# Moving the head, the softmax and the first projections of an attention layer, and ending its last block and the last row in halves of 256 tokens

## The chip, the cores and the metric

One NeuronCore of a Trainium2 chip runs the whole program. The metric is device time in microseconds for one execution. Engines are named as in the profile: PE (TensorE matmul), PEld (its weight loads), DVE (VectorE), ACT (ScalarE), POOL (GpSimd), SP (SyncE, which here only issues DMAs). Each engine works through its own list of instructions in order and waits for others by semaphores.

## The reference, cut to what matters

Four transformer layers over 2048 tokens of width 128, all float32. The kernel cuts the tokens into four rows ("b") of 512. The parts that matter here:

```
x = x + 0.5 * L0_ffn(layernorm(x))        # top-2 of 8 experts + a shared one
x = x + L0_attn(layernorm(x))             # 16 heads of 64, rope on q and k
x = x + 0.5 * L0_ffn(layernorm(x))
... layers 1 and 2, first half and attention of layer 3 ...
x = x + 0.5 * L3_ffn(layernorm(x))        # last thing computed

L0_attn(x):  h = layernorm(x) * ln_scale + ln_bias
             c_q, c_kv = h @ w_down_q.T, h @ w_down_kv.T        # 64 wide
             q, k, v   = c_q @ w_up_q.T, c_kv @ w_up_k.T, c_kv @ w_up_v.T
             q, k      = rope(q), rope(k)
             out       = softmax(q k.T / 8) v @ w_out.T + x
L3_ffn(x):   xr, xk = mu * x + (1 - mu) * x_of_the_token_before
             out    = sigmoid(xr @ W_r.T) * (relu(xk @ W_k.T)**2 @ W_v.T)
```

## The kernel before

**Stages.** The first mixture of experts sorts the tokens of all rows by expert into DRAM (`sorted_x`), works through tiles of 128 sorted tokens two at a time (`tiles`, lines 689 to 787: transpose L713, up L723, product L730, limits L732/L736, L737, L739, transpose L748, down L756, store L760), and gathers the results back per row (`back`, an indirect DMA on POOL at L804 and an add at L799). Layer 0's attention (`l0_attn_quick`) follows, then the second mixture, and so on up to the attention of layers 2 and 3 (`padded_attn_quick`) and the last layer's channel mix (`l3_ffn`).

**Layer 0's attention.** 32 steps, four rows of eight pairs of heads. A step computes the scores of its pair in four tiles of 128 keys (L1032, two 512-wide matmuls each), their exponentials on ACT (L1033 into `pT`), the products with the values (L1046), the running sums for the softmax's denominators on DVE (L1038, L1041: three 1024-wide additions) and a copy of the result on ACT (L1118 into `U`). Between the third and the fourth score tile it also projects the pair two steps ahead (L1014 on PE, copy L1016 on ACT into `qk`, then two DMAs L1019 that write the pairwise swapped rows into `other`) and turns the pair one step ahead on DVE (two multiplications by the rope table at L1024, an addition at L1025). The first two projections and the first turn stand ahead of the loop, at lines 1074 and 1075; their tiles come from the pool `work` of this stage.

Three further streams are generators, of which a `yield` ends a piece; the loop runs one piece in the middle of a step and one at its end:

- `l0_begin(b + 1)`, the head of the next row: two layer norms, the projections `w_down` to `cT` (L989 on PE, copy L991 on ACT) and V (L995, L997). It is appended at the end of the step `hp == NP - 6`, the third of the row; whatever is left of it runs in full before the first projection of the next row (`finish(chain(*begins))`), in the seventh step.
- `end(b)`: the sums of the denominators (L1052), the reciprocal (L1054), `watch` (L962, one pass that looks for overflow), spreading over partitions (L1062), four multiplications of `U` (L1064), the projection `w_out` (L1069) and the addition to x (L321).
- `late(b)`, the routing of a finished row for the second mixture: layer norm, transposes (L310), gate logits (L484), the softmax over 8 experts (`exps`, L354 to L357), ranks (L333 to L338), `taken` (L493), counts on PE (L500, L502), places, and eight indirect DMAs.

**Order of the work.** In this stage PE's list is exactly the order in which the code issues (`manual_schedule` on PE). The lists of DVE, ACT, POOL and SP are ordered by a scheduler that estimates times. PSUM holds three `big` tiles of two banks and two `one` tiles; a pool of the next stage lies over the memory of the last one (`reuse_waits="tile"`), so the first writer of a tile waits for the last users of what lay there.

**The last row.** In `padded_attn_quick` the step `end(k, U)` (L1465 denominators, L1467 reciprocal, L962, L1474, L1476, L1481) is followed for the last row by `l3_ffn` (layer norm L286 to L299, transposes L310, copy L1772, token mix L1778/L1779, L1784, L1786, L1788, L1791, L1792, L1796, L1797, L1798, and the store L1800), each operation over all 512 tokens.

Of the kernel before, what the change touches and what calls it, by code (L numbers as in the profile page):

```python
# [238 lines left out]
def program(ctx: ExitStack, tc: tile.TileContext, a: dict, out: bass.AP, worst):  # L239
# [193 lines left out]
    def by_expert(w, rooms, key):  # L433
# [33 lines left out]
        def route(b, work, rows_pool=None, slow=False):  # L467
# [6 lines left out]
            yield  # L474
# [8 lines left out]
            for t in range(NT):  # L483
                nc.tensor.matmul(lg[:, t, :], lhsT=xnT[:, t * P : (t + 1) * P], rhs=w["gate_w"], start=True, stop=True)  # L484
            sc = exps(lg, NT)
# [491 lines left out]

    def l0_begin(b, w, work, made, bufs):

        xa = keep.tile([P, NT, D], F32, tag="xn", name="xa", bufs=3)  # L980
        yield from layernorm_parts(x[b], xa)
        nc.gpsimd.tensor_tensor(x[b], x[b], xa, ALU.add)
        yield from layernorm_parts(xa, xa)
        yield
        hT = keep.tile([P, S], F32, tag=f"xnT{b}", name=f"hT{b}")
        nc.vector.tensor_scalar(hT, transposed(xa), w["ln_scale"], w["ln_bias"], ALU.mult, ALU.add)
        yield
        pd = one()
        nc.tensor.matmul(pd, lhsT=w["w_down"], rhs=hT, start=True, stop=True)  # L989
        cT = work.tile([P, S], F32, tag="cT", name="cT", bufs=bufs)  # L990
        nc.scalar.copy(cT, pd)  # L991

        pv = one()
        for t in range(NT):
            nc.tensor.matmul(pv[:, t * 64 : (t + 1) * 64], lhsT=hT[:, t * P : (t + 1) * P], rhs=w["w_down"][:, 64:128], start=True, stop=True)  # L995
        V = work.tile([P, NT, 64], F32, tag="V", name="V", bufs=bufs)
        nc.vector.tensor_copy(V.rearrange("p t d -> p (t d)"), pv[:, : NT * 64])  # L997
        made[b] = cT, V
        yield

    def l0_attn_quick(w, work, made, early, late):

        rope = w["c_rope"].rearrange("p (m s) -> p m s", m=2)
# [5 lines left out]

        def project(hp, cT):  # L1010

            pq = big()
            for k, row in enumerate((0, 64)):
                nc.tensor.matmul(pq[:, k, :], lhsT=w["w_up_qk"][row : row + 64, hp * P : (hp + 1) * P], rhs=cT[row : row + 64, :], start=True, stop=True)  # L1014
            qk = work.tile([P, 2, S], F32, tag="qk", name="qk", bufs=3)
            nc.scalar.copy(qk, pq)  # L1016
            other = work.tile([P, 2, S], F32, tag="other", name="other", bufs=2)
            for m in range(2):
                nc.sync.dma_start(out=other[m::2], in_=qk[1 - m :: 2])  # L1019
            return qk, other  # L1020

        def turned(qk, other):
            for v, m in ((qk, 0), (other, 1)):
                nc.vector.tensor_tensor(v, v, rope[:, m, :].unsqueeze(1).to_broadcast([P, 2, S]), ALU.mult)  # L1024
            nc.vector.tensor_tensor(qk, qk, other, ALU.add)  # L1025
            return qk[:, 0, :], qk[:, 1, :]
# [21 lines left out]
        def end(b, U, sums):  # L1048
# [5 lines left out]
            nc.vector.reciprocal(r, pz)  # L1054
            watch(b, pz, r)
            yield
            for k in range(2):
                for c2 in range(2):
                    pr = big()
                    for m in range(2):  # L1060
                        c = 2 * c2 + m
                        nc.tensor.matmul(pr[:, m, :], lhsT=spread[32 * c : 32 * c + 32, k, :], rhs=r[32 * c : 32 * c + 32, :], start=True, stop=True)  # L1062
                    u = U[k][:, 2 * c2 : 2 * c2 + 2, :]
                    nc.vector.tensor_tensor(u, u, pr, ALU.mult)  # L1064
                yield
# [8 lines left out]
        raw = {n: project(n, made[0][0]) for n in range(2)}  # L1074
        qk = {0: turned(*raw[0])}
# [14 lines left out]
        for n, (b, hp) in enumerate(todo):  # L1090
# [6 lines left out]
            for half in range(2):  # L1097
                pTs.append(work.tile([P, 2, 2, S], F32, tag="pT", name="pT", bufs=3))
                for t in (2 * half, 2 * half + 1):
                    if t == NT - 1 and n + 1 < len(todo):  # L1100
                        if n + 2 < len(todo):
                            b1, hp1 = todo[n + 2]
                            if hp1 == 0:
                                finish(chain(*begins))
                            raw[n + 2] = project(hp1, made[b1][0])
                        qk[n + 1] = turned(*raw[n + 1])
                    score(t, *qk[n], pTs[half])
# [21 lines left out]
            if b + 1 < B and hp == NP - 6:  # L1129
# [267 lines left out]
    def padded_attn_quick(rows, w, work, before, side):  # L1397
# [85 lines left out]


# [6 lines left out]
        for r in range(2 * len(todo) + 1):  # L1491
# [8 lines left out]
            if r:  # L1500
# [11 lines left out]
                if h1:  # L1512
                    nc.vector.tensor_copy(U[:, g1, :], po)  # L1513
                    if g1 == NG - 1:
                        ends.append(end(k1, U))
                        step(ends[0])
# [9 lines left out]
        finish(chain(*ends))  # L1526
# [293 lines left out]
    with tc.tile_pool(name="w0", bufs=1, reuse_waits="tile") as wp:  # L1820
# [9 lines left out]
        else:  # L1830
# [13 lines left out]
            with tc.tile_pool(name="work", bufs=1, reuse_waits="tile") as work:  # L1844
# [25 lines left out]
                first, second = chain(places, mix.back(0, wp), l0_begin(0, w0, head, made, 1)), mix.back(1, wp)  # L1870
# [15 lines left out]
            with tc.tile_pool(name="work", bufs=1, reuse_waits="tile") as work:  # L1886
                with tc.manual_schedule(engines={mybir.EngineType.PE}):
                    rest = l0_attn_quick(w0, work, made, [iter(())] + [mix.back(b, wp) for b in range(2, B)], lambda b: mix2.route(b, wp, slow=(b < B - 1)))
# [21 lines left out]
    with tc.tile_pool(name="w13", bufs=1, reuse_waits="tile") as wp:  # L1910
# [50 lines left out]
        else:  # L1961
            deep[0] = 3
            rows = [(n, b, causal) for n, causal in (("l2", True), ("l3", False)) for b in range(B)]
            with tc.tile_pool(name="work", bufs=1, reuse_waits="tile") as work:
# [11 lines left out]
                plan += [(4 + b, 8, channels(True, b)) for b in range(B)]  # L1976
# [21 lines left out]
                padded_attn_quick(rows, wa, work, before, side)  # L1998
                before(8)
# [17 lines left out]
```

## Time and profile before

| | |
|---|---|
| runs before | 1462.82, 1467.87, 1468.65 us; median 1467.87 us |
| profiled execution | 1463.96 us, span 1462.2 us, mean granted clock of PE 0.927 |
| PE / DVE / ACT / POOL busy | 87% / 66% / 44% / 19% of the span |
| layer 0's attention, first score to the last row's `w_out` | 213.5 to 581.8 us |
| last row, from the last copy into `U` to the store's issue | 1421.7 to 1451.1 us |

The profile is one execution. Its page gives busy shares of each engine, the span cut into 40 slices, the chain of work that ended last, and groups of instructions by line. A busy share is an average: what an edit is worth is read at its place, from which wait ends last there. "PEclk" is the share of its full clock that PE was granted.

### The profile page before, as it was taken

Reading aid. Unit: us, or ns where it says so; the run is one execution under the profiler, and the core shown is the slowest. Engines: PE = TensorE matmul, PEld = TensorE weight load, DVE = VectorE, ACT = ScalarE, POOL = GpSimd, SP = SyncE. Lnnn points to the kernel's source line nnn. Section 1 sums busy time; section 2 is a strip of 40 time slices with the busy share of each in tenths; the row PEclk is TensorE's granted clock in tenths of the full one; section 3 lists DMA queues with packets and bytes.
Section 4 is the critical chain, followed back from the end, with each engine's and each line's share of the span. In section 5 each row is a group of like instructions: output and inputs, shape, how many; then the busy total and the mean of one; then the engine's idle time right before and its main releaser. Section 6 shows DMA issues by size and latency. Waiting matters only on the chain.

```text
span 1462.2 us, 20126 instructions
## 1 busy us (share of the span) xinstructions
PE 1271.6 (87%) x7044; PEld 672.8 (46%) x7044; DVE 963.8 (66%) x2331; ACT 645.8 (44%) x920; POOL 284.6 (19%) x270
## 2 busy tenths in 40 slices
PE   6999879998999999999876598789897889899983
PEld 3555543343344434555544385453464445333322
DVE  4796769988888794977675646467666634364423
ACT  2445446544444451555543242434343445445550
POOL 3510420203112020202343212220213030210000
PEclk9999999999999998999996697799898999899996
DMA  7123111101111010022115000010010000000000
GB/s 271 42 72 98 52 63 73 72 29 57 65 44 59 29 67 25 30 62 64 30 37 178 1 1 1 30 30 1 7 31 22 1 14 24 22 1 15 1 8 10
DMA packets 59953, 63.52 MB, mean 43 GB/s; under 512 B 11066, under 2 KB 51267, under 8 KB 59203
## 3 DMA queue, kind: packets, MB, share of 16 engines
q1 hardware_dynamic: 54212, 50.60, 10.2%
q0 software_dynamic: 5632, 11.55, 2.7%
q8 instruction: 59, 0.97, 0.3%
q14 instruction: 50, 0.41, 0.1%
HBM read 28.69 MB, written 16.65 MB: 31 GB/s over the span
## 4 chain that ended last, share of the span: by engine, by line
PE 65%; DVE 17%; issue 8%; ACT 4%; POOL 3%; DMA 2%; SPq 0%; POOLq 0%; ACTq 0%; DVEq 0%
PE big L1032 7%; PE big L1446 6%; PE big L723 6%; PE one L1046 6%; PE one L1459 5%; PE big L568 3%; PE one L1069 2%; ACT pT L1449 2%; PE one L1481 2%; PE big L1014 2%; PE one L310 2%; PE one L756 2%; POOL rs L290 1%; PE big L1720 1%; PE one L1734 1%
## 5 line engine op out<-in xcount | busy, mean ns | idle before, releaser
L1449 ACT ACTIVATE pT<-big 128x1024 f32<-128x1024 f32 (+3 forms) x256 | 205.0, 866 | 235.5 <-PE big L1446 232.6
L1446 PE MATMUL big<-qkq,qkk 32*128 32x512 f32 (+3 forms) x1024 | 176.5, 580 | 23.8 <-ACT pT L1449 13.2
L290 POOL TENSOR_TENSOR rs<-rs,root 128x4 f32<-128x4 f32 x52 | 58.0, 1117 | 501.3 <-DVE rs L289 474.6
L1033 ACT ACTIVATE pT<-big 128x1024 f32<-128x1024 f32 x128 | 125.9, 1034 | 66.0 <-PE big L1032 65.1
L723 PE MATMUL big<-w_w,xsT 128*128 x312 | 152.0, 610 | 0.7 <-issue 0.3
L1032 PE MATMUL big<-qk 64*128 64x512 f32 x512 | 129.8, 624 | 12.5 <-DVE qk L1025 7.3
L1459 PE MATMUL one<-pT,V 128*32 128x512 f32 (+3 forms) x1024 | 121.3, 561 | 1.3 <-DVE pT L1453 0.9
L1046 PE MATMUL one<-pT,V 128*64 128x512 f32 x512 | 116.9, 598 | 0.0
L1446 PEld LDWEIGHTS big<-qkq,qkk 32*128 32x128 f32 x1024 | 64.3, 194 | 111.9 <-ACT pT L1449 43.9
L804 POOL DMA_INDIRECT yg<-sorted_y,ito x64 | 70.1, 1096 | 210.4 <-DMA sorted_y<-ys 152.4
L548 POOL DMA_INDIRECT sorted_x<-xn,irows x64 | 69.6, 1088 | 79.1 <-issue 22.0
L1032 PEld LDWEIGHTS big<-qk 64*128 64x128 f32 x512 | 47.9, 193 | 79.9 <-issue 54.0
L1041 DVE TENSOR_TENSOR sums<-sums,pT 128x1024 f32<-128x1024 f32 x64 | 78.2, 1221 | 5.7 <-ACT pT L1033 1.0
L1453 DVE TENSOR_TENSOR pT<-pT,w_c_tri 128x256 f32<-128x256 f32 x128 | 51.9, 422 | 35.4 <-ACT pT L1449 34.2
L723 PEld LDWEIGHTS big<-w_w,xsT 128*128 128x128 f32 x312 | 54.2, 194 | 39.4 <-issue 39.3
L1046 PEld LDWEIGHTS one<-pT,V 128*64 128x64 f32 x512 | 33.9, 136 | 73.6 <-issue 69.0
L1459 PEld LDWEIGHTS one<-pT,V 128*32 128x32 f32 x1024 | 29.5, 115 | 76.4 <-issue 55.6
L1513 DVE COPY U<-one 128x512 f32<-128x512 f32 x32 | 22.0, 689 | 63.9 <-PE one L1459 63.5
L730 DVE TENSOR_TENSOR us<-big,t1s 128x1024 f32<-128x1024 f32 (+1 forms) x40 | 47.7, 1193 | 24.0 <-PE one L713 20.4
L321 DVE TENSOR_TENSOR x<-x,one 128x512 f32<-128x512 f32 x32 | 21.9, 685 | 62.0 <-PE one L1069 19.5
L568 PE MATMUL big<-xnT,w_w 128*128 128x512 f32 x128 | 60.0, 607 | 2.1 <-DVE u L573 2.1
L1118 ACT COPY U<-one 128x512 f32<-128x512 f32 x32 | 18.8, 586 | 97.1 <-PE one L1046 97.1
(311 smaller groups left out, 2313.7 us busy)
## 6 DMA issues: line engine op xcount, KB each, us to landing
other<-qk SPq DMA_DIRECT2D x64, 256.0 KB, 2.4
xs<-sorted_x SPq DMA_DIRECT2D x78, 64.0 KB, 1.8
sorted_y<-ys SPq DMA_DIRECT2D x38, 128.0 KB, 1.8
w_w<-in_w SPq DMA_DIRECT2D x2, 2048.0 KB
w_l_w<-in_l_w SPq DMA_DIRECT2D x2, 2048.0 KB, 14.4
X<-pair_x SPq DMA_DIRECT2D x3, 512.0 KB, 3.6
pair_y<-y SPq DMA_DIRECT2D x6, 256.0 KB, 2.3
w_w<-in_w SPq DMA_DIRECT2D x1, 1152.0 KB, 15.0
```

The lines of the kernel that those rows point to most:

```text
L290: nc.gpsimd.tensor_tensor(rs, rs, root, ALU.pow)
L548: apart(nc.gpsimd.indirect_dma_start(out=sorted_x[:, :], out_offset=bass.IndirectOffsetOnAxis(ap=irows[:, b, j, t : t + 1], axis=0), in_=x ...
L568: nc.tensor.matmul(pa[:, m, :], lhsT=w["w13"][:, NE, m, odd, c * P : (c + 1) * P], rhs=xTs[b], start=True, stop=True)
L723: nc.tensor.matmul(pa[:, k, :], lhsT=st[u]["xT"][:, k * P : (k + 1) * P], rhs=w["w13"][:, bass.ds(st[u]["e"][k], 1), m].rearrange("p o a b ...
L804: nc.gpsimd.indirect_dma_start(out=y, out_offset=None, in_=sorted_y[: done(b) * P, :], in_offset=bass.IndirectOffsetOnAxis(ap=ito[:, b, j, ...
L1032: nc.tensor.matmul(sT[:, u, :], lhsT=k[r, t * P : (t + 1) * P], rhs=q[r, :], start=True, stop=True)
L1033: nc.scalar.activation(pT[:, :, t % 2, :], sT, AF.Exp, scale=scale)
L1041: nc.vector.tensor_tensor(s, s, pT[:, :, m, :], ALU.add)
L1046: nc.tensor.matmul(po[r, :], lhsT=V[:, t, :], rhs=pT[:, u, t % 2, :], start=(t == 0), stop=(t == NT - 1), tile_position=(0, 64 * u))
L1446: nc.tensor.matmul(sT[j // 2][:, j % 2, :n], lhsT=kT[r, t * P : (t + 1) * P], rhs=qT[r, S - n :], start=True, stop=True)
L1449: nc.scalar.activation(pT[j2][:, :, :n], sT[j2][:, :, :n], AF.Exp, scale=scale)
L1459: nc.tensor.matmul(po[32 * j : 32 * j + 32, S - n :], lhsT=V[k % 2][:, t, NJ * g + j, :], rhs=pT[j // 2][:, j % 2, :n], start=(t == 0), st ...
```

## The change

1. `project` and `turned` become `l0_project` and `l0_turned`, with their tiles `qk` and `other` in the pool `head`, which lives from before the first mixture. The first two projections and the first turn are issued as pieces of the chain that runs beside the first mixture's tiles, behind `l0_begin(0)`; the scheduler places the second pair's turn there too.
2. `l0_begin(b + 1)` is appended one step later (`NP - 5`), so its last piece falls to the forced finish ahead of the next row's first projection.
3. In a slow `route`, the piece boundary that stood between the layer norm and the transposes goes behind the gate logits: transposes and logits are each issued half a step earlier, and the softmax starts one piece after the logits.
4. In `end`, `watch` goes behind the multiplications; for the last row, the reciprocal, the spreading and the multiplications are done in two halves of 256 tokens.
5. For the very last row, `end` and `l3_ffn` are replaced by `end_all`, which does all of it in two halves of 256 tokens, and stores each half by its own DMA.

```diff
@@ route
             yield from layernorm_parts(x[b], xn)
-            yield
+            if not slow:
+                yield
             xnT = keep.tile([P, S], F32, tag=f"xnT{b}", name=f"xnT{b}")
 ...
+            if slow:
+                yield
             sc = exps(lg, NT)
@@ end of l0_attn_quick
             r = work.tile([P, S], F32, tag="rsum", name="rsum")
-            nc.vector.reciprocal(r, pz)
-            watch(b, pz, r)
+            N = S if b + 1 < B else S // 2
+            cols = [slice(n, n + N) for n in range(0, S, N)]
+            for n in cols:
+                nc.vector.reciprocal(r[:, n], pz[:, n])
             yield
-            for k in range(2):
-                for c2 in range(2):
 ...
+            for n in cols:
+                for k in range(2):
+                    for c2 in range(2):
 ...
+                    if k and n == cols[-1]:
+                        watch(b, pz, r)
+                    yield
@@ l0_attn_quick
-        raw = {n: project(n, made[0][0]) for n in range(2)}
-        qk = {0: turned(*raw[0])}
+        raw, qk = first
 ...
-            if b + 1 < B and hp == NP - 6:
+            if b + 1 < B and hp == NP - 5:
@@ padded_attn_quick
-                    if g1 == NG - 1:
+                    if g1 == NG - 1 and k1 + 1 < len(rows):
 ...
-        finish(chain(*ends))
+        before(len(rows))
+        end_all(len(rows) - 1, U)
@@ program, beside the first mixture's tiles
+                def projected():
+                    raw, qk = pair01
+                    for n in range(2):
+                        raw[n] = l0_project(n, made[0][0], w0, head)
+                        yield
+                    qk[0] = l0_turned(w0, *raw[0])
+                    yield
+
-                first, second = chain(places, mix.back(0, wp), l0_begin(0, w0, head, made, 1)), mix.back(1, wp)
+                first, second = chain(places, mix.back(0, wp), l0_begin(0, w0, head, made, 1), projected()), mix.back(1, wp)
```

The new `end_all`, shortened:

```
for c in cols:                       # two halves of 256 tokens
    pz = one(); 4 matmuls (pick); r[:, c] = 1 / pz; z[:, c] = pz (ACT)
for c in cols:
    for g2 in range(2): pr = big(); 2 matmuls (spread); U[..., c] *= pr
for i in range(2):                   # w_o, addition, statistics, POOL's power
    po = one(); 8 matmuls; x += po; bn_stats, bn_aggr x2; rs
for i in range(2):                   # normalise, transpose, copy
    xn (DVE x2); 2 transposes; xnT[:, half] (ACT)
for i in range(2):                   # token mix: 4 DVE operations
    ...
for i in range(2):
    pkr = big(); W_k (256 wide), W_r x2; relu and tanh (ACT); kT * kT (DVE)
for i in range(2):
    pv = one(); W_v x2; r, x (DVE); store of the half
watch(2 * B + b, z, r)
```

## The prediction

> **What bounds the kernel now.** I read the page first, then PE's waits inside layer 0's attention, then the chain of waits at the places that the change touches, then stretches around those places. The page gives the frame:
>
> ```profile
> PE 1271.6 (87%) x7044; PEld 672.8 (46%) x7044; DVE 963.8 (66%) x2331; ACT 645.8 (44%) x920; POOL 284.6 (19%) x270
> PEclk9999999999999998999996697799898999899996
> ```
>
> PE is the bound nearly everywhere, so an edit is worth the idle time of PE that it removes, plus what that idle time does to the clock. The waits of PE between 205 and 590 us, longest in total first:
>
> ```profile
> PE one L500 <- DVE taken L493: 8.8, 3, 4.2
> PE big L1032 <- DVE qk L1025: 7.3, 1, 7.3
> PE big L1062 <- DVE rsum L1054: 5.6, 4, 3.5
> PE big L1032 <- DVE U L1064: 5.2, 3, 1.7
> ```
>
> Each is a place of the change: the routing's counts waiting for the ranks, the first score waiting for the first turned pair, the spreading waiting for the reciprocal. The chain of waits shows the second and the last end, and the end of the program:
>
> ```profile
> 207.09 2.36 DMA other<-qk
> 213.51 5.05 PE big L1032 x12
> ...
> 562.36 3.37 DVE rsum L1054
> 565.77 5.16 PE big L1062 x16
> 570.93 2.86 PE one L1069 x12
> 573.79 1.71 PE big L568 x2
> 575.50 6.30 PE one L1069 x52
> ...
> 1422.85 3.37 DVE rsum L1467
> 1426.27 2.10 PE big L1474 x8
> 1429.67 5.63 PE one L1481 x32
> ```
>
> Stretches (columns: PE, PEld, DVE, ACT, POOL busy, then PEclk) show what idling costs afterwards:
>
> ```profile
> 340.90:344.30 3.40, 0.68 (x4) 0.00 (x0) 3.33 (x6) 0.58 (x1) 0.73 (x1) 1.00 0.05 19
> 344.30:351.10 6.80, 5.34 (x20) 3.98 (x22) 5.75 (x16) 0.00 (x0) 1.06 (x1) 0.50 0.04 10
> 887.00:890.40 3.40, 1.45 (x12) 1.36 (x12) 2.21 (x13) 0.69 (x1) 2.53 (x3) 1.00 0.00 0
> 890.40:897.20 6.80, 6.07 (x16) 3.35 (x14) 3.88 (x21) 0.58 (x1) 4.27 (x3) 0.50 0.02 4
> 323.60:360.00 36.40, 32.21 (x148) 14.60 (x146) 31.36 (x64) 16.89 (x21) 8.23 (x8) 0.91 0.14 51
> 1421.70:1451.10 29.40, 14.99 (x67) 9.94 (x66) 14.29 (x30) 1.67 (x3) 1.01 (x1) 0.75 0.00 1
> ```
>
> After 3.4 us with PE 0.68 us busy the clock is half for 6.8 us. The second pair of lines shows the same after 3.4 us with PE 1.45 us busy, 43%.
>
> **The change part by part.** Sums are against the profiled execution, 1463.96 us (3.9 below the median of the runs, 1467.87).
>
> *Entry of the attention (edit 1).* Removed: PE's wait of 7.29 us (206.22 to 213.51), made of the copy (1.02), the swap's issue and DMA (0.55 + 2.36), and the turn (1.23 + 1.15 + 1.24). It set the clock to half from 211.2 to 218.0; 4.5 us of scores ran in that, worth 2.2. Gross 9.5. The moved instructions all remain: on PE 1.99 us of L1014, on ACT two copies of 1.02, on SP four DMA issues ahead of later tile stores (L760, hidden: 0.56 each, the stores are waited for two units later at the earliest), on DVE six operations of 1.22, 7.3 us. From 169.0 to 206.2 PE was busy 36.3 of 37.2 us, DVE 25.6, ACT 16.8, so the room on DVE is 11.6 us. But DVE goes in order, and in the new list it stands at the first rope multiplication until the swap has landed. I place it: down-projection once hT is there (170.4), cT at 171.9, projection done near 174.2, copy to 175.2, swap landed near 178.4 (the old pair took 3.3 us from copy to L1024); the next tile product behind it (L730) has its matmuls only at about 180.8, so the wait and the first two multiplications just fit. From there five units of 3.5 us each, eight adds L799 of 0.33, four statistics, and 4.9 us of turning end DVE's last L739 near 208.2 instead of 201.2. PE, at its last L748, waits about 2 us for that, and loses 1.3 us earlier (the down-projection now directly follows the transposes L310 and waits for hT, where two L723 covered it). The first exponential, after the table load that stands in front of it (1.28), comes at about 211.4 instead of 216.95. Net 5.5. From both sides: 9.5 if DVE keeps up, 1 if every moved DVE microsecond lands on PE. I take 5.5, from the placing.
>
> *Routing and head (edits 2 and 3).* The waits at L500 are 4.19, 4.05 and 0.54 us, in rows 0, 1 and 2. They exist because from 333.3 to 341.6 DVE is full (8.30 of 8.30 us): the next row's second layer norm sits among softmax and ranks. With the softmax half a step earlier (into DVE's idle 2.34 us before L354) and the head a step later, I place `taken` at 337.8, ahead of L500 at 341.6. All 8.8 us go. So do the half clocks behind them: 5.35 and 5.7 us of PE work ran at half, worth 5.5. Gross 14.3. What is late next: the head's last piece is now forced ahead of L1014 in the seventh step. There L989 must be copied to cT (L991, 0.63) behind three running exponentials before L1014 can start; with exponentials ending 1.2 us behind the scores, PE waits 0.85 us in each of three rows, 2.6. It is covered only by L995 (0.5 to 1.0). DVE total in 323.6 to 360.0 is 31.4 of 36.4 us; without the gaps about 30 us of time remain there, so it fits only because the head's 5 us move behind 360, where DVE has 5.7 us free to 387.3. For such tightness I take off 1.
>
> *Ends of rows 0 to 2 (edit 4).* Taking `watch` (0.68 + 0.14) from behind the reciprocal frees the first multiplication 0.45 us sooner, but the scheduler now puts a rope multiplication (1.22) between the two: the second PSUM tile is freed 0.75 later, and the next multiplications about 1.3 later, which L1069 feels by 0.7. Bounds: gain 0.8 or loss 1.2 a row; I take a loss of 0.9, 2.7 in all. Edits 2 to 4 up to here: 14.3 - 2.6 - 1 - 2.7 = 8.
>
> *End of the last block (edit 4).* No row shows half sizes. A 512-wide L730 took 0.68, a 1024-wide one 1.22, so 256 more columns cost 0.27 and each instruction about 0.15. Half a reciprocal is then 1.75, half a multiplication 0.69. PE starts spreading at 564.1 instead of 565.8, but eight multiplications and `watch` (now third) end on DVE at 572.3, exactly as before. The last spreading needs a PSUM tile from the fifth multiplication, so L1069 starts at 570.7 instead of 570.9. What is gained: two L568 (1.71) leave the middle (0.9 comes back later at full clock), and some half clock (566.1 to 576.4 before). 1.5; bounds 0 and 3.6.
>
> *Last row (edit 5).* From the copy (1421.7) to the store (1451.1) were 29.4 us with DVE busy 14.3 and PE 15.0: a chain, hardly overlapped. In halves, by the same per-instruction costs: denominators to 1422.5, reciprocals to 1426.05, four multiplications with `watch` and the final check to 1430.05. With PE at full clock the first half's addition is at 1430.5, its normalised x at 1433.15 (POOL's 1.0 stalls DVE, with the other half queued behind it); the second half's addition 1433.6, POOL done 1436.2, transposes 1437.2, copy 1437.6, mix 1438.65, relu 1439.65, W_v 1441.1, end 1442.0: 9.1 saved. With PE at half, the second half's `w_o` ends at 1435.4 and the end is at 1444.85: 6.2 saved.
>
> **Two rules of the Trainium skill.** For the clock: "TensorE: Matmul & The Clock Gate", part 1, says half rate comes after one *idle* window of about 3.4 us. Halving leaves no idle window, so by the rule both ends run at full clock: 3.6 and 9.1. The row at 887.0 (43% busy, then half) says a half-busy window is enough, and both halved ends leave PE between 40 and 55% busy; by it 0.7 and 6.2. I go between, nearer the row: 1.5 and 7.5. Against the change, "VectorE: DVE Perf Modes", section on the TRN2 errata, advises tiles of 512 elements or more because each instruction pays a fixed latency. The 0.15 us above is that cost here; some 24 more DVE instructions in the two ends make 3.6 us if DVE were the bound throughout. In the last row it is busy half the time, so the rule costs only what the placing already contains; if obeyed (no halves), the two ends would bring 0.8 for the moved `watch` instead of 9.
>
> **Sum.** 5.5 + 8 + 1.5 + 7.5 = 22.5: 1441.5 us as the profiled execution counts. The runs shown lie up to 4.7 above it, so I put the forecast 1.5 higher, at 1443. No edit touches the stretch from 630 to 1405; it shifts as a whole, with clock windows falling elsewhere (2 us either way).
>
> **The rivals.**
>
> - *As summed* (0.65): 1435 to 1451.
> - *The clock stays full and nothing new waits* (0.12): entry 9.5, rows 14.3, ends 3.6 and 9.1, 36 at the most, some 30 likely: 1434. For it: PE's gaps at the ordinary ends (0.72 + 1.75 us) left the clock alone. Against: cT's wait follows from the order.
> - *DVE becomes the bound* (0.20): the moved turn lands on PE (1), DVE at 85% in the attention takes back most of the routing's gain (3), ends 0 and 6: 10 saved, 1454 to 1457, seen from the runs about 0.8% faster; with the tail at 4 it counts as the same.
> - *Slower* (0.03): the wait for the swap inside the tile loop. It is one DMA wait at the head of DVE's queue, with the tile products, L739 and so PE's L748 behind it. Beyond the 3.3 us that I took, each further microsecond costs one, since the cover up to 180.8 is used up. It decides from 22 us late; swaps here landed in 2.4 us each, tile stores in 1.8, so nothing speaks for it.
> - That the code does not do what it says: both programs' instruction lists show the first scores ahead of the last tile's L748, so it does.
>
> **How the numbers follow.** 0.5%, 7.3 us, is about what a measurement of this kernel can tell from no change (the runs spread over 5.8 us). Faster: 0.65 + 0.12 + 0.14 of the third case. Same: its remaining 0.06. Slower: 0.03. The range 1431 to 1455 takes in the first case with its bounds, most of the second and the better half of the third.
>
> **What would show it.** In the profile after: no PE wait at L500; a new wait of about 0.9 us, three times, of the projection for cT; the first exponential near 211; a tail of 20 to 23 us from the last copy into `U` to the store's issue, instead of 29.4; the last `w_out` of layer 0 ending within 20 us of its denominators. Wrong would be: a tile stage lengthened by more than 5 us, PE idle in the attention still above 20 us, or half clock through the whole tail.

## The result, and the profile after

The changed kernel takes 1446.1 us (median of four runs, 1444.26 to 1453.75) against 1467.3 us on the same chip: ratio 0.987, 95% interval 0.984 to 0.991. The forecast was 1443.0 us. The profiled execution took 1446.64 us with a span of 1444.9, 17.3 less than before. Line numbers behind the change are those of the new kernel, mostly a few higher (L1032 is now L1035).

The page of the kernel after, PE's line of part 1 and the clock of part 2:

```profile
PE 1273.6 (88%) x7078; PEld 674.7 (47%) x7078; DVE 963.1 (67%) x2348; ACT 648.8 (45%) x925; POOL 288.8 (20%) x271
PEclk9999899999999998999987698799798999989997
```

PE is busy as long as before (1271.6 us then) in a span 17.3 us shorter; what went, on balance, is idle time. PE's waits inside layer 0's attention after the change (engine, tile, line, what ended the wait; us in total, how many, longest):

```profile
PE big L1035 <- DVE U L1071: 6.8, 6, 1.1
PE big L1069 <- DVE rsum L1061: 4.0, 4, 1.9
PE one L759 <- ACT hTs L753: 1.1, 1, 1.1
PE big L985 <- ACT pT L1036: 0.8, 1, 0.8
```

The 8.8 us for the ranks (now L503) and the 7.3 us for the first turned pair are gone. One wait has become longer, the first line here: at the ends of rows the scores wait for a PSUM tile, 5.2 us in three waits of 1.7 before, now 6.8 in six of 1.1. The last two lines are new and small, both from the entry: the last tile's copy, and the first exponentials. In this profile no half-rate stretch begins between 184 and 549 us, where there were three (211.2, 344.3, 439.8).

The same marks in both traces (starts or ends of the same instruction) give the account of the 17.3 us:

| stretch | before | after | difference | predicted |
|---|---|---|---|---|
| to the first exponential (0.5 of it a later start already at 162 us) | 216.95 | 214.61 | -2.3, entry -2.9 | -5.5 |
| first exponential to row 0's denominators | 70.36 | 70.34 | 0 | 0 |
| row 0's denominators to row 3's | 271.35 | 258.66 | -12.7 | -8 |
| row 3's denominators (end) to its last `w_out` | 19.49 | 17.77 | -1.7 | -1.5 |
| from there to the ninth up matmul of the second tile stage | 48.60 | 52.53 | +3.9 | 0 |
| from there to the last copy into `U` | 791.33 | 794.33 | +3.0 | 0, 2 either way |
| last copy into `U` (start) to the last DVE instruction | 30.00 | 22.84 | -7.2 | -7.5 |

The remaining 0.3 us of the 17.3 lies behind the last DVE instruction. The parts had been summed to 22.5. That the total came out near the forecast is in part luck, since errors cancelled: the rows gave 4.7 us more than predicted, the entry 2.6 less, 3.9 us were given back right behind the last block, where the prediction had nothing, and 3.0 more went in the stretch that no edit touches.

### The profile page after: what moved, and what is told of

Read it like the earlier page. It is cut to its first block, busy times and chain, and to the rows that moved or that the text cites. A ratio compares the mean times of both kernels' runs of the same rounds, so it can differ in the third digit from the quotient of the medians.

```text
span 1444.9 us, 20212 instructions
## 1 busy us (share of the span) xinstructions
PE 1273.6 (88%) x7078; PEld 674.7 (47%) x7078; DVE 963.1 (67%) x2348; ACT 648.8 (45%) x925; POOL 288.8 (20%) x271
## 4 chain that ended last, share of the span: by engine, by line
PE 63%; DVE 16%; issue 10%; ACT 4%; POOL 4%; DMA 3%; POOLq 0%; SPq 0%; ACTq 0%; DVEq 0%
PE big L1035 8%; PE one L1049 7%; PE big L1454 6%; PE one L1467 5%; PE big L726 5%; PE big L571 2%; PE one L1078 2%; ACT pT L1457 2%; PE big L985 2%; PE one L1489 2%; PE big L1813 1%; PE one L310 1%; POOL rs L290 1%; PE one L1827 1%; PE one L759 1%
## 5 line engine op out<-in xcount | busy, mean ns | idle before, releaser
L1035 PE MATMUL big<-qk 64*128 64x512 f32 x512 | 126.6, 605 | 6.8 <-DVE U L1071 6.8
L1035 PEld LDWEIGHTS big<-qk 64*128 64x128 f32 x512 | 46.3, 186 | 69.3 <-issue 41.0
L733 DVE TENSOR_TENSOR us<-big,t1s 128x1024 f32<-128x1024 f32 (+1 forms) x40 | 47.7, 1193 | 21.5 <-PE one L716 19.7
L571 PE MATMUL big<-xnT,w_w 128*128 128x512 f32 x128 | 59.6, 601 | 1.4 <-DVE u L576 1.4
## 6 DMA issues: line engine op xcount, KB each, us to landing
w_w<-in_w SPq DMA_DIRECT2D x1, 1152.0 KB, 14.3
```

The source lines that it names most:

```text
L571: nc.tensor.matmul(pa[:, m, :], lhsT=w["w13"][:, NE, m, odd, c * P : (c + 1) * P], rhs=xTs[b], start=True, stop=True)
L1035: nc.tensor.matmul(sT[:, u, :], lhsT=k[r, t * P : (t + 1) * P], rhs=q[r, :], start=True, stop=True)
```

## The experiments

The experiments ran on three chips, where the kernel before took 1485.4 us (first four experiments), 1480.9 (the changed kernel again, without the new ends, fillers in the block, head back) and 1469.3 (the other three). Only ratios to the kernel before on the same chip are compared; traces are compared stretch by stretch. In the first four runs one part of the change stands alone on the kernel before; in the others the changed kernel is altered.

### Entry alone

```diff
-        raw = {n: project(n, made[0][0]) for n in range(2)}
-        qk = {0: turned(*raw[0])}
+        raw, qk = first
...
-                first, second = chain(places, mix.back(0, wp), l0_begin(0, w0, head, made, 1)), mix.back(1, wp)
+                first, second = chain(places, mix.back(0, wp), l0_begin(0, w0, head, made, 1), projected()), mix.back(1, wp)
```

> The kernel before with the first projections and the first turn moved into the tile stage, and nothing else. Theory (A): the entry brings about 2.8 us, not the 5.5 of the prediction, because ACT's table load for the exponential stands in order behind the last tile's two copies (first exponential near 214.3, before 216.95), although the first scores are there at 211. The reciprocal of row 0 comes about 2.9 us earlier and the whole is 2 to 4 us faster. Rival (B): the entry alone brings its 5.5, and the other edits took part of it in row 0; then the first exponential is near 211.4 and the whole 5 to 6 us faster.

Measured: 1484.2 against 1485.4 us, ratio 0.999 (0.997 to 1.001). From the first up matmul of the first mixture's tiles to the first exponential it takes 125.3 us; in the three kernels on the same chip that keep the old entry 128.2, 126.4 and 128.2. The gain at that mark is 1.1 to 2.9 us: rival B's 5.5 falls, and the runs don't tell this part from nothing.

The gain is not steady either. In the first pair of profiles this stretch went from 126.0 to 123.2 us; in the second profile of the changed kernel (the section on it stands below) it is 127.1, and 127.8 with fillers in the block, on the same chip. In both the last tiles make PE wait longer, and half rate is back under the first scores (second profile: from 213.5 to 220.4, after a window with PE 2.05 of 3.4 us busy). Over all profiles without the early table load the seven with the new entry average 125.1 us, the four with the old one 127.2.

### Routing and head alone

```diff
-            yield
+            if not slow:
+                yield
...
+            if slow:
+                yield
             sc = exps(lg, NT)
...
-            if b + 1 < B and hp == NP - 6:
+            if b + 1 < B and hp == NP - 5:
```

> The kernel before with the routing's softmax and the head in their new places, and nothing else. Theory (A): the new order costs no wait for cT (the down-projection itself, 1.0 us, covers the lag of the exponentials, and the V projection of 1.0 us covers the copy), so rows 1 and 2 each become 6.7 us shorter and row 3 about 1.8, 15 in all at row 3's denominators; of it some 3 to 5 are lost again between 580 and 630, where DVE sets the pace. Whole: 10 to 13 us faster. Rival (B), the terms of the prediction: three waits of 0.85 for cT and 1 us of DVE tightness, 10.7 at row 3's denominators.

Measured: 1470.7 us, ratio 0.990 (0.988 to 0.993), 14 us. From row 0's denominators to row 3's it takes 258.7 us; in the two kernels on the same chip that keep the old routing and the old row ends, 270.4 and 274.1. There is no wait for the ranks and none for `cT`. Theory A holds for the order of the work, and its total was a little too low: the 3 to 5 us that it saw lost behind the block were not (51.6 us from the last `w_out` to the ninth up matmul, 52.3 and 52.7 in those two kernels).

### Ends of layer 0 alone

```diff
-            nc.vector.reciprocal(r, pz)
-            watch(b, pz, r)
+            N = S if b + 1 < B else S // 2
+            cols = [slice(n, n + N) for n in range(0, S, N)]
+            for n in cols:
+                nc.vector.reciprocal(r[:, n], pz[:, n])
...
+                    if k and n == cols[-1]:
+                        watch(b, pz, r)
```

> The kernel before with the ends of layer 0 in their new form (halves in the last block, the check of the denominators behind the multiplications), and nothing else. Theory (A): each of the ends of rows 0 to 2 gets 0.5 us longer (1.6 in all), the last end 2 us shorter up to its last output projection; between 580 and 630, where DVE sets the pace, most of that is lost. Whole: no difference to be measured, from 1 us faster to 2 us slower. Rival (B): the last end keeps its gain (1.5 or more) and the three ends cost 0.9 each: 1 us slower. Rival (C): PE stays at full clock through the halved end: 2 us faster.

Measured: 1491.0 us, ratio 1.003 (1.001 to 1.006): 5 us slower, more than any of the three theories had. This part of the change loses. The last `w_out` does come earlier (17.2 us behind its denominators, 19.3 to 19.5 in the other three), but the next stretch, up to the ninth up matmul of the second tile stage, takes 56.3 us against 51.6 to 52.7. Rows 1 and 2 take 98.1 and 98.7 us against 94.5 to 96.1 with the old routing: more than the 0.5 us of waits, here the clock also fell to half for 3.4 us behind the ends of rows 0 and 1.

### Last row alone

```diff
-                    if g1 == NG - 1:
+                    if g1 == NG - 1 and k1 + 1 < len(rows):
...
-        finish(chain(*ends))
+        before(len(rows))
+        end_all(len(rows) - 1, U)
```

> The kernel before with the last row's end in halves, and nothing else. Theory (A): from the last copy into U to the store's issue 22 us instead of 29.4, with half clock in part of it: 7 us faster, and nothing before 1405 moves by more than the 2 us of clock windows. Rival (B): the 7.2 us seen with all edits together came from clock windows that happened to fall well; here the tail takes 24 us or more, or 20.3 where they fall better.

Measured: 1476.2 us, ratio 0.992 (0.989 to 0.995): 9 us by the medians, 12 by the ratio. From the last copy into `U` to the last DVE instruction it takes 22.2 us, in the other three kernels 30.1 to 31.0. Theory A for the tail, on another chip and with other clock windows. What the run may have beyond these 8 us would lie in stretches that the edit doesn't touch; there is no trace of the kernel before on this chip to place it.

### The changed kernel again, and without the new ends

For the second, `end` is the old one:

```diff
-            N = S if b + 1 < B else S // 2
-            cols = [slice(n, n + N) for n in range(0, S, N)]
-            for n in cols:
-                nc.vector.reciprocal(r[:, n], pz[:, n])
+            nc.vector.reciprocal(r, pz)
+            watch(b, pz, r)
...
```

> The changed kernel as it is, run again beside the others so that all have one chip for comparison. The parts alone gave ratios of 0.999 (entry), 0.990 (routing and head), 1.003 (ends of layer 0) and 0.992 (last row), product 0.985. If the parts add up, the whole is 0.985 (0.983 to 0.987); if routing and entry cover the same idle time, 0.990.

> The changed kernel with the ends of layer 0 put back into their old form (full width in the last block, check of the denominators ahead of the multiplications). Theory (A): that part of the change loses time. From row 3's denominators to the ninth first-layer matmul of the second tile stage it made 70.3 us of 68.1 (the end 1.7 us shorter, what follows 3.9 us longer), and each of the other three ends at least 0.5 us longer. Undone, the kernel is 3 to 6 us faster than the changed one. Rival (B): the loss seen in that part alone comes from its meeting with the old routing, and beside the new routing it is worth the 1.5 us of the prediction; undone, the kernel is 1 to 2 us slower. Rival (C): 0, within 1 us.

Measured: the changed kernel 1463.0 us, ratio 0.988 (0.985 to 0.991), the same ratio as in the first comparison and within noise of the product of the parts (0.985). Without the new ends 1453.4 us, ratio 0.982 (0.979 to 0.985). From row 3's denominators to the ninth up matmul the traces have 74.6 against 71.6 us. The three ends of rows have 1.75 instead of 2.28 us of waits each behind the spreading, but the rows are no shorter for it (258.64 against 258.60 us from row 0's denominators to row 3's): in one of them half rate followed, for 3.4 us. In the untouched stretch up to the last copy into `U` the two profiles differ by 9.7 us (802.7 and 793.1), and there the clock was half for 163.8 and 143.4 us; 20.4 us more of it cost a busy PE 10.2, so that difference is the clock's. The runs show the loss, 3.0 us of the 9.6 can be placed, and the rest stays unassigned. Theory A.

### Only the check of the denominators back in its place

```diff
             for n in cols:
                 nc.vector.reciprocal(r[:, n], pz[:, n])
+            if N == S:
+                watch(b, pz, r)
             yield
...
-                    if k and n == cols[-1]:
+                    if k and n == cols[-1] and N < S:
```

> The changed kernel with the check of the denominators ahead of the multiplications again in rows 0 to 2; the halves in the last block stay. It splits the loss of that part. Theory (A): the place of the check costs 0.53 us at each of three ends (two waits of 1.14 us for PSUM tiles in place of one of 1.75), the halves cost 3.0 us up to 630. The three ends go back to one wait of 1.75, the stretch from row 3's denominators to the ninth first-layer matmul of the second tile stage stays at 74.5 us, and the whole is 1.6 us faster than the changed kernel. Rival (B): all of the loss lies in the check's place: then the stretch falls to 71.5 too and the whole is 4 us or more faster.

Measured: 1444.9 us, ratio 0.983 (0.980 to 0.986), against 0.987 and 0.988 for the changed kernel in the other comparisons. Three waits of 1.75 us are back, and the stretch from row 3's denominators is 70.2 us, as in the first profile of the changed kernel (70.3; 74.5 was the value of the second chip). So in waits the check's place costs 0.53 us at each of three ends, and the halves cost what follows the last block: theory A in the traces. The ratio fell further than its 1.6 us, and the traces don't show by what. Nor are the rows shorter (258.6 us, as in the changed kernel): one wait of 1.75 leaves a window 49% busy, behind which half rate came at the end of row 0, while the two waits of 1.14 fell into two windows, each 67% busy. The chain of waits at the end of row 0, first the changed kernel:

```profile
293.92 1.13 DVE qk L996
295.05 1.13 DVE U L1071
296.18 1.13 DVE other L996
297.31 1.14 DVE U L1071
298.46 0.04 issue
298.50 1.13 PE big L1035 x4
```

and this version:

```profile
293.72 0.33 DVE one L965
294.05 0.27 issue
294.32 0.14 DVE worst L965
294.46 1.08 DVE qk L996
295.54 1.14 DVE U L1073
296.68 0.04 issue
296.73 3.67 PE big L1035 x7
```

DVE's list is ordered by a scheduler. In the changed kernel two rope multiplications (L996) stand between the multiplications of `U` that free PSUM tiles, with the check ahead of them only one.

What the halves cost begins with order too. `made`, the first step of sorting the tokens for the second mixture, is a small DVE instruction. Its row in the kernel before, in the changed kernel and in the last but one experiment below (old ends); the column behind the durations gives the start of the first and of the second mixture's instruction:

```profile
L618 DVE TENSOR_TENSOR made<-allb,w_c_room x2: 171/172/172, 69.2 to 606.1; 128x32 f32<-128x32 f32 x2
```

```profile
L621 DVE TENSOR_TENSOR made<-allb,w_c_room x2: 171/176/181, 69.7 to 592.8; 128x32 f32<-128x32 f32 x2
```

```profile
L621 DVE TENSOR_TENSOR made<-allb,w_c_room x2: 173/173/173, 69.3 to 582.5; 128x32 f32<-128x32 f32 x2
```

The addition to `x` behind the last `w_out` is at 581.8, 565.1 and 558.3 us. With whole ends `made` comes 24.2 us later, with halves 27.8, and so it is in all thirteen profiles (seven with whole ends, six with halves). In between DVE is busy for 20.9 and 23.5 us, on the routing and on the shared expert's units (lines 576 to 584 after the change). Of those unit operations 23 stand between the addition and `made` with whole ends (14.2 us of DVE), 27 with halves (16.9 us): four more ahead of the sorting make 2.7 of the 3.5 us. That the scheduler placed them so because its estimates moved with the halves is likely and not shown.

Counted from row 3's denominators, where the whole ends lose 1.7 us up to the addition, `made` is 1.8 us later, and in this pair of profiles PE's first transposes of the sorted rows (L713, now L716) only 0.4. The larger part of the loss here is the clock's. PE's first wait for the sorted rows is 0.6 to 0.9 us with whole ends and 1.7 in all six profiles with halves. The windows around it before (55% busy, then full rate) and, second pair, after (44% busy, then half rate):

```profile
620.80:624.20 3.40, 1.87 (x7) 0.84 (x5) 3.20 (x12) 1.61 (x4) 0.00 (x0) 1.00 0.20 58
624.20:627.60 3.40, 2.94 (x19) 2.30 (x20) 3.40 (x26) 0.05 (x1) 0.00 (x0) 1.00 0.27 77
607.80:611.20 3.40, 1.48 (x9) 1.12 (x10) 3.40 (x22) 1.00 (x2) 0.00 (x0) 1.00 0.28 77
611.20:614.60 3.40, 3.40 (x13) 2.62 (x13) 2.99 (x25) 0.37 (x1) 0.00 (x0) 0.51 0.27 80
```

So the 3.9 us behind the last `w_out` are 1.7 of half rate, 0.6 of longer waits, and 1.1 for two matmuls of the next stage (L571) that stood ahead of it before; 0.5 stays open. How much half rate falls there varies: PE works 0 to 3.4 us at half rate in this stretch with whole ends, 3.4 to 6.7 with halves. On each chip the stretch from row 3's denominators to the ninth up matmul is longer with halves, by 1.8 to 2.8 us on average (the combined kernel with its fillers left out).

### Fillers in the last block's wait

```diff
+            if N < S:
+                pf = big()
+                for _ in range(2):
+                    nc.tensor.matmul(pf[:, 0, :], lhsT=w["w_down"], rhs=w["w_up_qk"][:, :S], start=True, stop=True)
             yield
```

> The changed kernel with two more matmuls (128x512, 1.02 us each, nobody reads the result) on PE in its wait of 1.88 us for the first half of the last block's reciprocals. Theory (A): the clock goes down because of the busy share of the window before, 0.45 in 546.4 to 549.8; filled, it stays full, and the 9.5 us of PE work in the next 10.2 us take 4.7 us less, so that the last output projection of layer 0 ends 13 us after the denominators instead of 17.8. By 630, where DVE sets the pace, 2 to 4.5 us of it are left. Whole: 2 to 4.5 us faster than the changed kernel. Rival (B): half clock there has another cause (only a window that is wholly idle, the load of the whole chip, the hour); the projection ends as late as before, and the matmuls cost 0.2 us. Rival (C): the clock stays full, but the chain on DVE behind it eats it all: 13 us and no change at 630.

Measured: ratio 0.988 (0.985 to 0.990), no difference; the last `w_out` ends 17.6 us after the denominators. The windows of this kernel (columns: PE, PEld, DVE, ACT, POOL busy, then PEclk):

```profile
548.40:551.80 3.40, 3.40 (x24) 1.16 (x18) 2.17 (x2) 0.00 (x0) 0.00 (x0) 1.00 0.00 0
551.80:555.20 3.40, 2.38 (x24) 1.24 (x16) 3.40 (x5) 0.00 (x0) 0.00 (x0) 1.00 0.05 5
555.20:562.00 6.80, 6.47 (x32) 5.26 (x29) 3.22 (x7) 0.00 (x0) 0.00 (x0) 0.50 0.01 2
```

The fillers made one window full, but the next, with the second wait (1.0 us) in it, was 70% busy, and half rate followed all the same. The experiment missed: it can't tell A from B, since it did not fill every window. The 70% speak against a sharp threshold at 46.

### The head back

```diff
-            if b + 1 < B and hp == NP - 5:
+            if b + 1 < B and hp == NP - 6:
```

> The changed kernel with the head of the next row begun a step earlier again (where it was before the change); the routing's new places stay. Theory (A): the head and the routing's ranks share DVE again, PE waits at the routing's counts (L503) in rows 0 and 1, 2 us or more each with a half-rate stretch behind it: rows 1 and 2 longer by 3 us each, the whole 4 to 7 us slower than the changed kernel. Rival (B): the softmax half a step earlier was enough by itself: no wait at L503, and no difference within 1 us. Rival (C), the prediction's 0.85 us a row for cT, hidden somewhere in the new order: 2 us faster.

Measured: 1461.8 us, ratio 0.987 (0.984 to 0.990), the same as the changed kernel. Rival B: the softmax's new place is enough. Whether the head's new place alone would have done as well was not run. What the head's place is worth in waits is this line of this kernel, two waits of 0.5 us:

```profile
PE one L503 <- DVE taken L496: 0.9, 2, 0.5
```

Its rows take 260.7 us against 258.6; 1.7 of that lies in row 3, where half rate came for 3.4 us at 482.2, behind two of the waits of 1.14 us. That the head's place brings this on is not shown.

### Old ends, early table load, fillers

```diff
+                    if warm and u == nu - 2:
+                        j = tiny.tile([P, 1], F32, tag="warm", name="warm")
+                        nc.scalar.activation(j, hT[:, 0:1], AF.Exp)
...
             watch(b, pz, r)
+            if b + 1 == B:
+                pf = big()
+                for _ in range(3):
+                    nc.tensor.matmul(pf[:, 0, :], lhsT=w["w_down"], rhs=w["w_up_qk"][:, :S], start=True, stop=True)
             yield
...
+            def fill(v):
+                pf = big()
+                nc.tensor.matmul(pf[:, 0, : v.shape[-1]], lhsT=w3["l3_wk"], rhs=v, start=True, stop=True)
+            fill(U[:, NG - 1, :])
```

Four such fills stand in the last row's end: behind the denominators, between the two spreadings, behind `w_o`, between the transposes.

> The changed kernel with the ends of layer 0 in their old form, and three additions: a one-column exponential right behind the copy of the second last tile (so that ACT loads its table in a gap), three matmuls of 1.02 us that nobody reads in PE's wait of 3.48 us for the last block's reciprocals, four such matmuls in the waits of the last row's end. Theory (A), half clock comes from a PE busy less than about 0.46 of a 3.4 us window: the first exponential comes 1.3 us earlier; behind the last block's denominators the clock stays full, and its last output projection ends 15 us after them instead of 19.4; the last row's end takes 20 us instead of 22.5. Against the version with the old ends alone 5 to 8 us faster, ratio to the kernel before 0.977. Rival (B): the fillers do nothing to the clock (they are as short of load as the work around them), 19.4 and 22.5 stay, 1 us faster or less. Rival (C): DVE, which sets the pace behind the last block, eats the 4 us there; 2 to 4 us faster.

Measured: 1434.7 us, ratio 0.976 (0.974 to 0.979), 1.1% below the changed kernel's ratio. The last `w_out` ends 15.6 us behind its denominators and the last row takes 19.7 us; on the same chip the kernel of the next section, which has the old ends and the table load but no fillers (and the head's old place, far from both marks), takes 19.0 and 22.8. Theory A for the clock. The windows of this kernel at the last block, and the last row:

```profile
542.60:546.00 3.40, 2.84 (x10) 1.05 (x6) 3.27 (x1) 0.00 (x0) 0.00 (x0) 1.00 0.00 0
546.00:556.30 10.30, 9.64 (x67) 6.92 (x68) 5.46 (x7) 0.00 (x0) 0.00 (x0) 1.00 0.03 3
1400.90:1420.60 19.70, 15.02 (x92) 9.21 (x92) 15.55 (x41) 2.81 (x8) 1.42 (x2) 1.00 0.02 7
```

and the same of the changed kernel:

```profile
546.40:549.80 3.40, 1.52 (x18) 0.64 (x12) 2.48 (x2) 0.00 (x0) 0.00 (x0) 1.00 0.00 0
549.80:560.00 10.20, 9.51 (x49) 7.16 (x44) 6.31 (x11) 0.00 (x0) 0.00 (x0) 0.50 0.01 2
1411.90:1434.70 22.80, 15.69 (x84) 11.45 (x84) 15.29 (x41) 2.80 (x8) 1.56 (x2) 0.76 0.02 6
```

The clock is full where it was half. Of the 3.4 us gained at the last `w_out`, 2.1 are left at the ninth up matmul (65.5 us after the denominators against 67.6 without fillers): the other 1.3 went to half rate, which came for 3.4 us at 600.7 in this kernel and not in that one, and not to DVE as rival C had it: PE idles 3.7 us behind the last `w_out` in both. This is the fastest of all kernels here.

### A smaller change

The old ends, the head's old place and the early table load; of the change are left entry, softmax and last row.

```diff
-            if b + 1 < B and hp == NP - 5:
+            if b + 1 < B and hp == NP - 6:
...
+                    if warm and u == nu - 2:
+                        j = tiny.tile([P, 1], F32, tag="warm", name="warm")
+                        nc.scalar.activation(j, hT[:, 0:1], AF.Exp)
...
```

> The changed kernel with the ends of layer 0 in their old form, the head of the next row where it was before the change, and the early table load; what is left of the change is the entry, the softmax's place and the last row. Theory (A): the head's new place brought nothing (undone beside the new ends: 1461.8 against 1463.0 us), the table load brings 1.3 us at the first exponential: same time as the version with the old ends alone or 1 us better, ratio to the kernel before 0.981. Rival (B): with the check of the denominators back in its place DVE meets ranks and head again: waits of PE at L503 of 2 us or more in rows 0 and 1, ratio 0.985 or more.

Measured: 1441.8 us, ratio 0.981 (0.978 to 0.985), the waits at L503 0.9 us in two. From the last tile's transposes (L751) to the first exponential 2.2 us, as in the version above; 3.6 in the changed kernel. Theory A: two of the change's five edits can be left out, and the kernel is no slower for it. By the ratio it is faster (0.987 and 0.988 for the changed kernel in the other comparisons); 1.4 us of that is the table load.

## Why the prediction was right, and where it was not

**Entry: the step that failed is "the first exponential, after the table load that stands in front of it (1.28), comes at about 211.4".** It came at 214.61. The chain of waits of the changed kernel there:

```profile
200.69 3.00 DMA yg<-sorted_y,ito
...
206.26 0.61 DVE hs L742
...
209.88 1.05 PE big L1035 x2
210.94 0.37 PE one L751 x2
211.30 1.05 PE big L1035 x2
212.36 0.66 PE one L759 x4
213.01 0.02 issue
213.03 0.27 ACT ys L761
213.30 0.02 issue
213.32 0.83 ACT L1036
214.15 0.46 issue
214.61 1.03 ACT pT L1036
```

The two waits counted in the tile stage were about right: 1.42 us for `hT`, 1.1 and 0.4 us at the end (predicted 1.3 and 2). DVE's last L742 ended at 209.4 instead of 208.2: DVE stood 0.35 us for a gathered row (the DMA at 200.69), and two copies of 0.7 us (L979), which before came behind the tiles' last product, now stand ahead of it. The larger error is behind it: PE has two scores of 1.05 us in its list ahead of the last tile's L751 and L759, and the table load stands in ACT's list behind that tile's last copy (L761). I had put the load where ACT was free, not where its list had it. The early load showed that 1.4 us of it can go. The prediction's 2.2 us for the clock came in this profile, but not in the second profile of the same kernel, where half rate returned at this place.

**Routing and head: gross right, two subtractions wrong.** Predicted 14.3 less 2.6, 1 and 2.7. The rows gained 12.7 with 1.6 of waits lost at their ends (three times 0.53, where I had put 0.9 a row): 14.3 gross. The combined kernel with old ends, whose rows have no half-rate stretch, takes 257.2 us there, 14.2 less than before. "PE waits 0.85 us in each of three rows" for `cT` was nothing:

```profile
349.39 2.78 PE big L1035 x12
352.17 1.06 PE one L1011 x2
353.22 0.84 PE one L1017 x8
354.06 1.06 PE big L985 x4
```

L1011, the down-projection itself, lasts 1.06 us, about what the exponentials lag behind; the copy to `cT` starts at 353.26 and ends at 353.84, and the V projection (L1017) covers it. I had counted the second cover and forgotten the first. The 1 us for DVE's tightness was nothing either, although DVE is full:

```profile
328.00:338.00 10.00, 10.00 (x46) 3.48 (x44) 9.76 (x22) 5.67 (x8) 0.00 (x0) 1.00 0.20 76
338.00:348.00 10.00, 10.00 (x52) 4.39 (x50) 9.86 (x28) 5.28 (x6) 3.13 (x2) 1.00 0.21 83
348.00:358.00 10.00, 10.00 (x48) 4.31 (x46) 9.86 (x14) 5.88 (x7) 8.11 (x6) 1.00 0.16 55
```

DVE at 98% for 30 us, and PE without a pause: the order of the work fits, so a full engine cost nothing here. And "it fits only because the head's 5 us move behind 360" was wrong: with the head back, two waits of 0.5 us were left.

**End of the last block: the size was right at the place, and the wrong place was summed.** 1.7 us came at the last `w_out` (predicted 1.5). The step that failed is that the stretch behind shifts as a whole: it grew by 3.9 us. I had let 0.9 for the two L568 come back; 1.1 came back, PE's wait for the sorted rows grew, and half rate followed it (1.7). From row 3's denominators to the ninth up matmul the halves lose 2.2 us in this pair of profiles. The ends of rows 0 to 2 add 1.6 of waits; with the old ends the rows were shorter by that only in the combined kernel (257.2 us). In runs this part loses more, 5 us alone and 9.6 when undone, and I had rated it 1.5 of gain less 2.7.

**Last row: right.** 22.2 us between the end of the last copy and the last update of `x`, predicted 7.5 less than 29.4. It is the case with half rate: the window 1413.4 to 1416.8 was 1.50 us busy, and `w_o` of the first half took 3.25 us against 2.00 in the kernel with fillers. The full-rate case, predicted at 9.1 saved, came out at 10.3 there (30.0 to 19.7), fillers included.

**The rule on the clock.** I weighed the row 887.0 (43% busy, then half rate) against the idle window of the Trainium skill ("TensorE: Matmul & The Clock Gate", part 1), and went near the row. The stretches of one clock in all thirteen traces are whole multiples of 3.41 us. Cut into windows of that length up to 1390 us, they agree with the row: of windows at full rate with PE under 40% busy all 203 were followed by half rate; between 40 and 50% 47 of 78; between 50 and 60% 23 of 55; above 60% 53 of some 4140. Back to full led no window under 80% busy, and 319 of 481 of those above 90%. So half rate comes well before a whole window is idle, and the fillers of the combined kernel show that PE's own load is the cause here and not a companion. What brings half rate after the 53 well filled windows stays open; the 70% window above is one.

**"VectorE: DVE Perf Modes"**, whose section on the TRN2 errata speaks against small tiles: the 0.15 us for an instruction held (halves of the multiplication took 0.67 us, 0.69 predicted). In the last row it cost nothing visible, in the last block the halves lost, but by order and the clock and not by that latency: DVE's total work was the same 963 us.

## What to carry to other kernels

A long wait is worth what it says, with the half-rate stretch behind it, where nothing takes its place: so it was for the routing (14.3 us forecast and found), while at the entry 9.5 us shrank to 2.9, because the moved work and the table load stood in the lists ahead of the first exponential. A next engine at 98% cost nothing here as long as the lists kept their order. Before an end is cut into halves to start something earlier, look at what the next stage waits for: here a small sorting step on another engine, whose place in the list the cut changed, and a wait of PE behind it, long enough for half rate. Where PE waits for 2 to 4 us, matmuls that nobody reads can keep its clock, if every 3.4-us window that the wait touches is well filled (80% and 86% held it here, 70% did not); and where ACT changes its function, look where in its list the table load stands.

## What the runs showed of the hardware

- The kernel before took 1467, 1485, 1481 and 1469 us in the four comparisons, nearly as much apart as the change is worth; each comparison ran on one chip, so chip and hour are not told apart. The stretch from the ninth up matmul to the last copy into `U` took 791 to 794 us in six profiles and 799 to 806 in seven, with the same instructions: in the first group the clock was half for 140 to 147 us of it, in the second for 157 to 167. Both groups occur on one chip.
- The share that separates best the windows followed by full and by half rate is 46% busy, with 99 of 4480 windows on the wrong side. Coming back asks for more than staying: a window at least 80% busy, and above 90% it came back in two of three.
- A busy PE is not always a loaded one. Of the 3398 windows at full rate that were over 90% busy, 29 were followed by half rate, and each of these 29 holds 1.1 to 2.1 us of matmuls with 8 columns (L1631, the gate of layer 2) or 9 rows (L538, the mixture's second biases). Of the 3251 such windows with under 0.5 us of them none was. No run changed these matmuls, so the cause is not shown.
- A row's end with 3.0 us of PE idle in three pieces (0.72, 1.14, 1.14) kept full rate in the changed kernel (the windows 79, 67 and 67% busy) and lost it in the kernel with the new ends alone (44% and 48% busy where two pieces fell together): whether the pieces fall in one window is decided by where the window begins.
